# A biased node table made in pieces of 512 nodes at every second pair, read from group 8 on

## The chip, the cores and the metric

The kernel runs on one core of one Trainium2 chip. The metric is device time in microseconds (us); lower is better. The time before the change is 4156.67 us, the median of three runs (4152.97 to 4159.75).

## What is computed

Two graph layers over 6250 nodes of 256 features and 200000 edges, whose destinations are sorted. The change touches the first one:

```python
e = edge_attr @ W_edge + b_edge                 # 200000 x 256
msg = relu(x[src] + e)                          # a gather of node rows
agg = segment_sum(msg, dst, num_segments=6250)
h = relu(((1 + eps) * x + agg) @ W1 + b1) @ W2 + b2   # then batch norm, relu, residual, layer norm
```

The second layer is an attention layer on the result (a gather of rows again, a softmax over each node's edges, a weighted sum). b_edge isn't zero.

## The kernel before

**Tiles, pairs and groups.** The edges are cut into 1563 tiles of 128 edges, one edge on a partition. 14 tiles make a group (112 groups, the last of 9 tiles), and two tiles make a *pair*, seven to a group, 782 in all. The first layer is one loop over the pairs (k from 0), whose order on VectorE (DVE), TensorE (PE), ScalarE (ACT) and SyncE (SP) is the order in which the code is written. GpSimd (POOL) only issues gathers.

**A pair.** `fetch` (L571 on) has POOL issue two indirect DMAs at L576, one for each tile, of 128 rows of 256 floats into a buffer xg; there are 14 such buffers. `features` multiplies the edge attributes by W_edge into PSUM (L586). `sums` adds the gathered rows to it on VectorE (L590) and so releases the xg buffer; `upper` (ScalarE, L595) and `lower` (VectorE, L599) apply the relu and split it into two parts, and `add_up` (TensorE, L609) sums the messages by destination with a one-hot matrix, which `hot` (VectorE, L557) makes for each group. Fetch and features run two pairs ahead of the sum, POOL as far ahead as its buffers and semaphores let it. At each group's end, `flush` runs over the following pairs: totals (L465, L466), and for every two groups the two-layer net and its statistics (L395 to L428).

**The bias.** The bias b_edge can enter in two ways. In groups below GB (XB_FROM = 6) the rows are gathered from the input x, and one more matmul per pair adds the bias (L584, three bf16 rows against a row of ones). In groups from GB on, the rows come from a table xb_tab = x + b_edge in HBM, and that matmul is left out.

**The table.** `first_table` (L515 on) makes it. A step loads 256 nodes from x (L529, SP) into one of three buffers xr, two rows of 1 KB on each partition, 128 nodes apart; then it adds the bias to the piece loaded two steps earlier (L534, VectorE, in place) and writes that piece out (L535, SP). There are 25 pieces (the last has 106 nodes) and 27 steps, one at the end of each pair from k = 4 on.

**What else is in these queues.** SP issues all DMAs that aren't gathers, in the order written, and waits in that order too: every two groups one load of edge attributes ea (L545, 1792 KB), every group a window xw of x (L512, 128 KB), and index loads of 70 KB. There are 13 parts of the indices. `positions` (L137, with the subtraction on VectorE at L131) makes the columns that `hot` needs; its parts 1 to 12 are stepped at every pair from k = 0, two pairs for each part. `order` (loads at L145 and L147, VectorE at L151 to L154) checks the order of the edges; it is stepped at every pair from group GB on. Both take their buffers from the pool ldp, which has two of each kind. `break_columns` (L270) later fills pen_f, a table of 1564 columns.

Of the kernel before, what the change touches and what calls it, by code (L numbers as in the profile page):

```python
# [6 lines left out]
F32 = mybir.dt.float32  # L7
# [4 lines left out]
OP = mybir.AluOpType  # L12
# [6 lines left out]
P = 128  # L19
S = 14  # L20
D = 256
# [8 lines left out]
SLOPE = 0.01  # L30
NEG = -1000.0
BIG = 1e30
XB_FROM = 6
RING = 5
YB = 8
SHORT = 6
# [14 lines left out]
def gnn(ctx, tc, io, N, E):  # L51
    nc = tc.nc
# [4 lines left out]
    GU = NSUB // S  # L57
    GB = min(XB_FROM, G)
    NB = -(-N // P)
# [14 lines left out]
    xb_tab = dram.tile([N, D], F32, name="xb_tab")  # L74
# [14 lines left out]
    be_bc = const.tile([P, D], F32, name="be_bc")  # L89
# [30 lines left out]
    pen_f = const.tile([P, NSUB + 1], F32, name="pen_f")  # L120
    RG = 10
    parts = [(0, 1)] + [(a, min(a + RG, GU)) for a in range(1, GU, RG)]
    parts = [(gs[a], gs[b], first[:, a:b]) for a, b in parts if b <= GU]
# [10 lines left out]
    def positions(r, pool):  # L134
        c0, c1, firsts = parts[r]
        dst_i = pool.tile([P, RG * S], I32, tag="dst_i", name="dst_i")[:, :c1 - c0]
        nc.sync.dma_start(dst_i, io["dst_p"][:, c0:c1])  # L137
        yield
        yield
        minus_first(dloc[:, c0:c1], dst_i, firsts)  # L140
# [40 lines left out]
    def load_rest():  # L181
        if G > 1:
            nc.sync.dma_start(src_sb[:, n0:], io["src_p"][:, n0:])
        nc.scalar.dma_start(w1_sb, io["W1"].rearrange("(k p) f -> p k f", p=P))
        nc.scalar.dma_start(w2_sb, io["W2"].rearrange("(k p) f -> p k f", p=P))
        nc.scalar.dma_start(cols, io["cols"].rearrange("p (a c) -> p a c", c=2))
        nc.scalar.dma_start(ope, io["eps"].partition_broadcast(P))
# [258 lines left out]

    with ExitStack() as st:
        gp = st.enter_context(tc.tile_pool(name="gp", bufs=14))
        ldp = st.enter_context(tc.tile_pool(name="ldp", bufs=2))
        wk = st.enter_context(tc.tile_pool(name="wk", bufs=2))  # L450
        hlp = st.enter_context(tc.tile_pool(name="hlp", bufs=4))
        eap = st.enter_context(tc.tile_pool(name="eap", bufs=2))
# [55 lines left out]
        def window(g):  # L508
            base = nc.values_load(gf_i[:1, g:g + 1], engines=[ET.SP], min_val=0,
                                  max_val=N - 1, skip_runtime_bounds_check_because=IN_RANGE)  # L510
            xw = wk.tile([P, D], F32, tag="xw", name="xw", bufs=3)
            nc.sync.dma_start(xw, io["x"][ds(base, P)])  # L512
            return xw

        def first_table():  # L515

            b_bc = be_bc.unsqueeze(1).to_broadcast([P, 2, D])
            todo = []
            for r0 in range(0, N, 2 * P):
                w = min(2, (N - r0) // P)  # L520
                todo += [(a0, a1, n) for a0, a1, n in
                         ((r0, r0 + w * P, P), (r0 + w * P, min(r0 + 2 * P, N), N % P)) if a1 > a0]
            loaded = []
            for i in range(len(todo) + 2):
                if i < len(todo):
                    a0, a1, n = todo[i]
                    xr = gp.tile([P, 2, D], F32, tag="xr", name="xr", bufs=3)
                    xr = xr[:n, :(a1 - a0) // n]
                    nc.sync.dma_start(xr, io["x"][a0:a1].rearrange("(b p) d -> p b d", p=n))  # L529
                    loaded.append(xr)  # L530
                if i >= 2:
                    a0, a1, n = todo[i - 2]
                    xr = loaded.pop(0)
                    nc.vector.tensor_tensor(xr, xr, b_bc[:n, :(a1 - a0) // n], op=OP.add)  # L534
                    nc.sync.dma_start(xb_tab[a0:a1].rearrange("(b p) d -> p b d", p=n), xr)  # L535
                yield

        def pieces(m):

            t0, t1 = gs[2 * m], gs[min(2 * m + 2, G)]  # L540
            ea_t = eap.tile([P, 2 * SP_], F32, tag="ea", name="ea_t")
            cuts = [0, 2, 8, t1 - t0] if m == 0 else [0, t1 - t0]
            for c0, c1 in zip(cuts, cuts[1:]):
                if c1 > c0:
                    nc.sync.dma_start(ea_t[:, c0 * P:c1 * P], io["eaT"][:, (t0 + c0) * P:(t0 + c1) * P])  # L545
            for t in range(t0, t1):
                EA[t] = ea_t[:, (t - t0) * P:(t - t0 + 1) * P]

        def hot(g):

            n = gs[g + 1] - gs[g]
            OH[g] = ohp.tile([P, S, P], F32R, tag="oh", name="oh")
            h = (n + 1) // 2
            for c0, c1 in ((0, h), (h, n)):
                if c1 > c0:
                    dl = dloc[:, gs[g] + c0:gs[g] + c1]
                    nc.vector.tensor_tensor(OH[g][:, c0:c1], iota_p.unsqueeze(1).to_broadcast([P, c1 - c0, P]),  # L557
                                            dl.unsqueeze(2).to_broadcast([P, c1 - c0, P]), op=OP.is_equal)
                yield
# [52 lines left out]
        K = len(pairs_)  # L612
# [4 lines left out]
        with tc.manual_schedule(engines={ET.DVE, ET.PE, ET.Activation, ET.SP}):  # L617
            def run(gen):
                for _ in gen:
                    pass  # L620

            run(positions(0, ldp))
            pieces(0)
            run(hot(0))
            load_rest()
            XW[0] = window(0)

            side = [positions(r, ldp) for r in range(1, len(parts))]
            rest = [first_table()]
            checks = [order(r, ldp) for r in range(len(parts))]  # L630
            hots, flushes = iter(()), []
            fill = zeros()
            extras = [place_rows(t0, pps, wk) for t0 in range(0, NSUB, P)]
            for f in (0, 1):
                if f < K:
                    fetch(f)
                    features(f)

            def step(queue):
                while queue:  # L640
                    if next(queue[0], True) is None:
                        return True
                    queue.pop(0)
                return False

            for k in range(K + 2):
                g = pairs_[min(k, K - 1)][0]
                if k < K and pairs_[k][1] == 0:
                    hots = hot(g + 1) if g + 1 < G else iter(())
                    if g % 2 == 0 and g + 2 < G:  # L650
                        pieces(g // 2 + 1)
                    if g + 1 < G:
                        XW[g + 1] = window(g + 1)
                    if g == GB - 1:
                        while step(rest):
                            pass
                j = k - firsts_[g] if k < K else 99
                if k + 2 < K:
                    fetch(k + 2)
                    features(k + 2)  # L660
                if k < K:
                    sums(k)
                    upper(k)
                    if 1 <= k:
                        lower(k - 1)
                elif k == K:
                    lower(k - 1)
                if k >= 2:
                    add_up(k - 2)
                    if k - 2 in lasts_:  # L670
                        run(fill)
                        gg = pairs_[k - 2][0]
                        flushes.append(flush(gg, ACC.pop(gg), XW.pop(gg)))
                        if gg > TG and extras:
                            flushes.append(extras.pop(0))
                if k == min(2, K - 1):
                    places_rest()
                if j >= 3:
                    next(hots, None)
                if k < K and pairs_[min(k + 1, K - 1)][0] != g:  # L680
                    run(hots)
                if k < 7:
                    next(fill, None)
                step(flushes)
                if len(flushes) > 1:
                    step(flushes)
                step(side)
                if 4 <= k < K and g < GB:
                    step(rest)
                if g >= GB:  # L690
                    step(checks)
                if k < K and g == TG and pairs_[k][1] == 0:
                    while step(side):
                        pass
                    while step(checks):
                        pass
                    flushes.append(tables(pps, wk))
                    extras = [break_columns(), break_rows(pps, wk)] + extras
            for q in (side, rest, checks, flushes, extras):
                while step(q):  # L700
                    pass
# [678 lines left out]
```

## Time and profile before

| | us |
|---|---|
| median of three runs | 4156.67 (4152.97 to 4159.75) |
| profiled execution, its own time | 4159.51 |
| its span | 4157.7 |
| busy: PE / DVE / ACT / POOL | 2891.7 / 3209.3 / 1029.3 / 3026.7 |
| DMA: read / written | 617.82 MB / 34.99 MB |
| mean granted TensorE clock | 0.824 |

A group line of the profile reads: line, engine, operation, tile written <- tiles read, count | busy us, mean ns of one | idle time of the engine just before them, and what ended it. A line of the timeline has the start, the duration, engine, line, operation, tiles and count, and in brackets the idle time before it with what ended it. A line of the waits has the engine and line that waited, what released it, the total in us, how often, and the longest. A line of the windows has the stretch, then the busy time (and count) of PE, PE's weight loads, DVE, ACT and POOL, the granted clock, the share of the DMA engines that was busy, and GB/s. The suffix q (SPq) marks what an engine's queue issues.

### The profile page before, as it was taken

How to read it: one execution, taken by the hardware profiler on the slowest of the kernel's cores; microseconds unless marked ns; L12 is line 12 of the kernel's file. 1: busy time of each engine (PE TensorE's matmuls, PEld its weight loads, DVE VectorE, ACT ScalarE, POOL GpSimd, SP SyncE). 2: the span in 40 equal slices, each digit the busy share in tenths (PEclk: the TensorE clock that was granted, in tenths of full speed). 3: DMA queues.
4: the chain of work that ended last, by engine and by line, in shares of the span. 5: the costliest groups of instructions: out<-in, count | busy, mean ns of one | idle time of the engine just before them, and what ended most of it. 6: DMA issues, size and time to landing. Idle time of an engine off the chain costs nothing. (4 is left out here: it accounts for less than half of the span.)

```text
span 4157.7 us, 46749 instructions
## 1 busy us (share of the span) xinstructions
PE 2891.7 (70%) x11765; PEld 2091.6 (50%) x11765; DVE 3209.3 (77%) x8203; ACT 1029.3 (25%) x2936; POOL 3026.7 (73%) x3158
## 2 busy tenths in 40 slices
PE   5678777777777777777736666666666666666665
PEld 3466555555566555555524444444444444444443
DVE  5788887777777777777747878787777888777787
ACT  2233333333333333333411111111111111111111
POOL 6577777777777777777457777777777777777773
PEclk8899899999989989999867777777777777777777
DMA  7555555555555555555555555555555555555552
GB/s 248 171 181 183 162 172 168 165 166 166 166 162 165 165 162 162 163 165 164 166 162 142 149 149 150 149 146 145 148 149 149 150 150 145 148 149 148 149 144 69
DMA packets 298114, 656.09 MB, mean 158 GB/s; under 512 B 86923, under 2 KB 170235, under 8 KB 290668
## 3 DMA queue, kind: packets, MB, share of 16 engines
q0 software_dynamic: 150144, 416.54, 36.3%
q1 hardware_dynamic: 146090, 235.43, 16.9%
q8 instruction: 98, 1.61, 0.2%
q14 instruction: 180, 1.47, 0.1%
q10 hardware_dynamic: 1602, 1.04, 0.1%
HBM read 617.82 MB, written 34.99 MB: 157 GB/s over the span
## 5 line engine op out<-in xcount | busy, mean ns | idle before, releaser
L912 POOL DMA_INDIRECT ring<-z_tab,src_sb x1563 | 1509.6, 966 | 495.3 <-issue 300.5
L576 POOL DMA_INDIRECT xg<-xb_tab,src_sb x1479 | 1402.1, 948 | 474.5 <-issue 303.6
L1049 PE MATMUL acc<-y,oh 128*128 128x260 f32 x3126 | 1132.0, 508 | 287.5 <-DVE y L1045 285.6
L586 PE MATMUL pt<-we_sb,ea_t 128*128 128x256 f32 x3126 | 919.4, 420 | 320.9 <-DVE hl L599 315.5
L1049 PEld LDWEIGHTS acc<-y,oh 128*128 128x128 f32 x3126 | 683.6, 242 | 509.4 <-DVE y L1045 387.5
L586 PEld LDWEIGHTS pt<-we_sb,ea_t 128*128 128x128 f32 x3126 | 605.6, 206 | 549.9 <-issue 294.0
L595 ACT ACTIVATE hl<-pt 128x512 fp32r<-128x512 f32 x782 | 467.1, 597 | 1116.7 <-DVE pt L590 1035.0
L590 DVE TENSOR_TENSOR pt<-pt,xg 128x512 f32<-128x512 f32 x782 | 540.6, 691 | 213.1 <-DMA xg<-xb_tab,src_sb 196.8
L609 PE MATMUL acc<-hl,oh 128*128 128x512 f32 x1563 | 690.4, 525 | 3.0 <-ACT hl L595 3.0
L599 DVE SCALAR_TENSOR_TENSOR hl<-pt,hl 128x512 fp32r<-128x512 f32 x782 | 530.8, 679 | 0.5 <-ACT hl L595 0.5
L1045 DVE TENSOR_TENSOR y<-ring,cst 128x520 f32<-128x520 f32 x782 | 520.4, 678 | 2.5 <-PE cst L1017 2.5
L609 PEld LDWEIGHTS acc<-hl,oh 128*128 128x128 f32 x1563 | 322.6, 207 | 55.3 <-ACT hl L595 3.8
L999 PE MATMUL tr<-consts,top 128*4 128x128 f32 x112 | 41.4, 370 | 407.2 <-DVE top L981 407.1
L961 PEld LDWEIGHTS <-ohT 128*128 128x128 bf16 x1563 | 176.8, 116 | 191.0 <-issue 88.6
L1063 ACT COPY ag<-acc 128x260 f32<-128x260 f32 x111 | 41.7, 376 | 868.1 <-DVE acc L1060 868.1
L557 DVE TENSOR_TENSOR oh<-iota_p,dloc 128x896 fp32r<-128x896 f32 x224 | 240.9, 1076 | 0.0
L970 DVE TENSOR_TENSOR oh<-cst,dloc 128x896 f32<-128x896 f32 x224 | 240.5, 1074 | 0.0
L999 PEld LDWEIGHTS tr<-consts,top 128*4 128x4 f32 x112 | 9.2, 82 | 414.8 <-issue 398.5
L989 DVE TENSOR_TENSOR e<-e,ring 128x56 f32<-128x56 f32 x112 | 28.4, 254 | 195.7 <-DMA ring<-z_tab,src_sb 195.0
L961 PE MATMUL pds<-edw,ohT 128*128 128x12 bf16 x1563 | 162.1, 178 | 17.2 <-DMA dlb<-dl_tab 15.2
L422 DVE SCALAR_TENSOR_TENSOR pmk<-p,mk 128x128 f32<-128x128 f32 x224 | 56.3, 289 | 117.9 <-ACT h2T L412 117.9
L395 PE MATMUL p<-hw,w_sb 128*128 128x256 f32 (+1 forms) x456 | 118.5, 384 | 5.2 <-DVE carry L480 4.6
(219 smaller groups left out, 2915.8 us busy)
## 6 DMA issues: line engine op xcount, KB each, us to landing
ea_t<-in_eaT SPq DMA_DIRECT2D x54, 1792.0 KB
dlb<-dl_tab SPq DMA_DIRECT2D x111, 448.0 KB
ring<-z_tab,src_sb POOLq DMA_INDIRECT x1563
xg<-xb_tab,src_sb POOLq DMA_INDIRECT x1479
xw<-in_x SPq DMA_DIRECT2D x112, 128.0 KB
hw<-hT_tab SPq DMA_DIRECT2D x112, 128.0 KB
out<-o SPq DMA_DIRECT2D x110, 128.0 KB
xr<-in_x SPq DMA_DIRECT2D x24, 256.0 KB
```

The lines of the kernel that those rows point to most:

```text
L557: nc.vector.tensor_tensor(OH[g][:, c0:c1], iota_p.unsqueeze(1).to_broadcast([P, c1 - c0, P]), dl.unsqueeze(2).to_broadcast([P, c1 - c0, P] ...
L576: nc.gpsimd.indirect_dma_start(out=XG[k][:, i, :], out_offset=None, in_=io["x"] if g < GB else xb_tab, in_offset=bass.IndirectOffsetOnAxis ...
L586: nc.tensor.matmul(pt[:, i, :], EA.pop(gs[g] + j0 + i), we_sb, start=not g < GB, stop=(not g < GB or i == w - 1))
L590: nc.vector.tensor_add(PT[k][:, :w], PT[k][:, :w], XG.pop(k)[:, :w])
L595: nc.scalar.activation(HL[k][:, :w, 0], PT[k][:, :w], AF.Relu)
L599: nc.vector.scalar_tensor_tensor(HL[k][:, :w, 1], PT.pop(k)[:, :w], 0.0, HL[k][:, :w, 0].bitcast(F32), op0=OP.max, op1=OP.subtract)
L609: nc.tensor.matmul(ACC[g].rearrange("p a d -> p (a d)"), OH[g][:, j0 + i], hl[:, i].rearrange("p a d -> p (a d)"), start=(j0 + i == 0), st ...
L912: nc.gpsimd.indirect_dma_start(out=zg[:, j, :], out_offset=None, in_=z_tab, in_offset=bass.IndirectOffsetOnAxis(ap=src_sb[:, t:t + 1], axi ...
L961: nc.tensor.matmul(pd[:, j].rearrange("p h c -> p (h c)"), ohT[:, j * P:(j + 1) * P], T["edw", g].bitcast(BF16)[:, :3 * H], start=True, st ...
L970: nc.vector.tensor_tensor(T["oh", g][:, c0:c1], iota_p.unsqueeze(1).to_broadcast([P, c1 - c0, P]), dloc[:, gs[g] + c0:gs[g] + c1].unsqueez ...
L1045: nc.vector.tensor_tensor(y[:, :w], T["zg", g][:, j0:j0 + w, :ZW].rearrange("p s (h f) -> p s h f", f=F + 1), by_edge(T["ex", g], g)[:, j0 ...
L1049: nc.tensor.matmul(T["acc", g].rearrange("p h f -> p (h f)"), T["oh", g][:, j0 + i, :], y[:, i].rearrange("p h f -> p (h f)"), start=(j0 + ...
```

## The change

- A piece of the table has 512 nodes (TB = 4), with four neighbouring nodes on a partition, so that a partition's part is one run of 4 KB in x and in the table. There are 12 such pieces and one of 106 nodes, 15 steps.
- A step is made at every second pair, from k = 2 to k = 30.
- Groups 6 and 7 still read x and add the bias on TensorE; the first group that reads the table is 8. The number of gathers from x is 112 instead of 84.
- Two xr buffers of 4 KB on a partition, and the first 1024 columns of pen_f as the third.
- The pool ldp has one buffer of each kind instead of two.
- After the first part, `positions` stands still until the table is done (the second part's load is issued at k = 2 and its subtraction is done after the table); then it goes on at every pair. `order` starts with group 8.

```diff
-XB_FROM = 6
+XB_FROM = 8
+TB = 4
+AHEAD = 2
...
-        ldp = st.enter_context(tc.tile_pool(name="ldp", bufs=2))
+        ldp = st.enter_context(tc.tile_pool(name="ldp", bufs=1))
...
-            b_bc = be_bc.unsqueeze(1).to_broadcast([P, 2, D])
-            todo = []
-            for r0 in range(0, N, 2 * P):
-                w = min(2, (N - r0) // P)
-                todo += [(a0, a1, n) for a0, a1, n in
-                         ((r0, r0 + w * P, P), (r0 + w * P, min(r0 + 2 * P, N), N % P)) if a1 > a0]
+            b_bc = be_bc.unsqueeze(1).to_broadcast([P, TB, D])
+            whole = N // (TB * P) * TB * P
+            todo = [(r0, r0 + TB * P, P, TB) for r0 in range(0, whole, TB * P)]
+            for r0 in range(whole, N, P):
+                todo.append((r0, min(r0 + P, N), min(P, N - r0), 1))
             loaded = []
-            for i in range(len(todo) + 2):
+            for i in range(len(todo) + AHEAD):
                 if i < len(todo):
-                    a0, a1, n = todo[i]
-                    xr = gp.tile([P, 2, D], F32, tag="xr", name="xr", bufs=3)
-                    xr = xr[:n, :(a1 - a0) // n]
-                    nc.sync.dma_start(xr, io["x"][a0:a1].rearrange("(b p) d -> p b d", p=n))
+                    a0, a1, n, b = todo[i]
+                    if i % (AHEAD + 1) == 0 and pen_f.shape[1] >= TB * D:
+                        xr = pen_f[:, :TB * D].rearrange("p (b d) -> p b d", b=TB)
+                    else:
+                        xr = gp.tile([P, TB, D], F32, tag="xr", name="xr", bufs=AHEAD)
+                    xr = xr[:n, :b]
+                    nc.sync.dma_start(xr, io["x"][a0:a1].rearrange("(p b) d -> p b d", p=n))
                     loaded.append(xr)
-                if i >= 2:
-                    a0, a1, n = todo[i - 2]
+                if i >= AHEAD:
+                    a0, a1, n, b = todo[i - AHEAD]
                     xr = loaded.pop(0)
-                    nc.vector.tensor_tensor(xr, xr, b_bc[:n, :(a1 - a0) // n], op=OP.add)
-                    nc.sync.dma_start(xb_tab[a0:a1].rearrange("(b p) d -> p b d", p=n), xr)
+                    nc.vector.tensor_tensor(xr, xr, b_bc[:n, :b], op=OP.add)
+                    nc.sync.dma_start(xb_tab[a0:a1].rearrange("(p b) d -> p b d", p=n), xr)
                 yield
...
-                step(side)
-                if 4 <= k < K and g < GB:
+                if len(side) >= len(parts) - 1 or not rest:
+                    step(side)
+                if 2 <= k < K and k % 2 == 0:
                     step(rest)
                 if g >= GB:
                     step(checks)
```

In the changed kernel the lines stand a little lower: the gather is L580, the bias matmul L588, the sum L594, the table's load, add and write L533, L538 and L539, positions L139 and L133, order L147, L149 and L153 to L156.

## The prediction

> **What bounds the kernel now.** I read the page first. Its line 4, the chain that ended last, says nothing here (four pieces, all at the very end), so I went by part 5 and by the waits.
>
> ```profile
> span 4157.7 us, 46749 instructions
> ...
> L912 POOL DMA_INDIRECT ring<-z_tab,src_sb x1563 | 1509.6, 966 | 495.3 <-issue 300.5
> L576 POOL DMA_INDIRECT xg<-xb_tab,src_sb x1479 | 1402.1, 948 | 474.5 <-issue 303.6
> ```
>
> POOL issues one gather per tile of 128 edges in each layer. A gather takes 0.948 us and about 0.30 us lies between two, so one starts every 1.25 us and a pair every 2.506 us. From 151.72 us to the last gather of the first layer (2003) POOL's timeline has no longer hole: (2002.1 - 153.0) / 738 pairs = 2.506. VectorE (77%) and TensorE (70%) follow POOL there, 3 us behind at the end. So what POOL loses before 151.7 moves the end of the first layer one to one, and the second layer (1563 gathers again) starts that much later. The next views are the windows and POOL's timeline.
>
> ```profile
> 100.00:150.00 50.00, 27.86 (x88) 16.72 (x86) 29.98 (x66) 9.52 (x25) 13.26 (x14) 0.78 0.66 196
> ...
> 200.00:250.00 50.00, 35.30 (x132) 25.10 (x133) 45.91 (x119) 16.00 (x41) 37.81 (x41) 0.93 0.62 199
> ```
>
> ```profile
> 85.16 0.94 POOL L576 DMA_INDIRECT xg<-in_x,src_sb  x1 [4.02 <-DVE pt L590]
> ...
> 126.75 0.95 POOL L576 DMA_INDIRECT xg<-in_x,src_sb  x1 [0.30 <-issue]
> 151.72 0.94 POOL L576 DMA_INDIRECT xg<-xb_tab,src_sb  x1 [24.03 <-DVE oh L557]
> ```
>
> The fifth column of the windows is POOL: 14 gathers in one 50 us, 41 in the other. Two kinds of hole make it. From 85 to 126 us, before the first gather of each of 11 pairs, POOL waits for an xg buffer (released by the sum, L590): 22.4 us together, 19.1 over the usual 0.30 each. Then 24.03 us before the first read of xb_tab, 23.7 over the usual: the last write of the table is issued at 146.5 and has to land; "DVE oh" is only what ended nearby. **Lost: 42.8 us**, and that is all that the change can win in the table's neighbourhood.
>
> Why the table is late is on SP:
>
> ```profile
> SPq L529 <- DMA xb_tab<-xr: 65.9, 22, 10.6
> ```
>
> ```profile
> 88.39 0.37 SPq L529 DMA_DIRECT2D xr<-in_x  x1
> 88.86 0.44 SPq L535 DMA_DIRECT2D xb_tab<-xr  x1
> 92.76 0.37 SPq L529 DMA_DIRECT2D xr<-in_x  x1
> 93.22 0.42 SPq L535 DMA_DIRECT2D xb_tab<-xr  x1
> 96.57 0.37 SPq L529 DMA_DIRECT2D xr<-in_x  x1
> ```
>
> With three buffers, the load of a step waits for the write issued just before it. One step is therefore one write's trip, 3.8 us (92.76 to 96.57), for each pair, against POOL's 2.5 us. VectorE does one add per pair in order, so its sums fall back to 3.8 us a pair, its lag uses up the 14 buffers (pair 30: sum at 135.5, gathered at 80.2), and POOL stops.
>
> **The change part by part.**
>
> *Steps at every second pair, 512 nodes each.* 13 steps of load instead of 25, the same bytes; a step now has two pairs, 5.0 us at POOL's pace. How long is it? No row shows a 512-node step. From below it is today's 3.8 us; from above twice that, 7.7. In between: the added 0.52 MB (load and write) move beside the gathers. The windows give 310 GB/s in 70 to 84 us, where a big ea load runs with the DMA engines 91% busy, and the gathers take 0.26 MB per 2.5 us = 105 of it; 0.52 MB at 205 GB/s is 2.6 us. I take **6.4 us**. The first add stays near 38 us (SP is held until 31.3 by an index load in both kernels); its write lands near 42.7, then nine steps to the last load, 57.6 us, and once an ea load in between (today the step at 72.14 lasts to 84.41: 8.5 us extra). The last load is issued at 109 and the sum of pair 30 runs at about 112. The last write, behind another ea load, lands by about 125.
>
> *First read in group 8.* Its first gather is number 112. On continuous gathers from 80.2 us (pair 30) that is 25 pairs later at 2.506, 143 us plus the port term below. The table is there some 20 us earlier: the 24.0 us wait goes. What is late next is the buffers.
>
> *Buffers.* POOL is held when a sum runs more than 14 x 2.506 - 1.25 - 0.96 = 32.9 us after its gather. Pair 30 in the new order: 112 - 84 = 28 (80.2 us plus some 4 of port delays). Pairs 30 to 56 carry the bias matmul; pairs 31 to 45 today (bias up to 41) took 146.3 to 181.9, 2.54 a pair, so 1 us is added. Pairs 56 to 82 carry the order checks; today's (42 to 68) took 175.9 to 246.1, 2.70 a pair, 5 us added. That is 34 at the worst place: about **1 us** over. With the step at 7.7 us the same sum is 39.5 + 6, 12.6 over; at 3.8 the adds on VectorE decide, 30, nothing over.
>
> *Bias matmuls in groups 6 and 7.* 14 more of L584 at 0.385 us with a weight load of 0.09: 6.7 us of PE, which idles (57% busy from 0 to 150 us). The 2.54 a pair above contains them. Nothing on POOL. If that cover is gone, it is at most 6.7 us.
>
> *The adds.* 24 of 0.69 us become 12 of about 1.25 (two 512-wide pieces of 0.60 and the drain); VectorE's total is unchanged. But look at what an add does to POOL:
>
> ```profile
> 54.24 0.69 DVE L534 TENSOR_TENSOR xr<-xr,be_bc 128x512 f32<-128x512 f32 x1 [1.08 <-DMA xr<-in_x]
> 54.68 1.06 POOL L576 DMA_INDIRECT xg<-in_x,src_sb  x1 [0.31 <-issue]
> ...
> 59.60 0.69 DVE L534 TENSOR_TENSOR xr<-xr,be_bc 128x512 f32<-128x512 f32 x1 [3.21 <-issue]
> 59.81 1.30 POOL L576 DMA_INDIRECT xg<-in_x,src_sb  x1 [0.30 <-issue]
> ```
>
> A gather that starts while an add runs is longer: 0.36 us with 0.48 us of the add left, 0.12 with 0.25 left (54.68, and again at 40.77). So the delay is what is left, less 0.13. Gathers start every 1.25 us, so an add of 1.25 us catches one each time, with 0 to 1.12 us to pay, on average 1.12 x 1.12 / 2 / 1.25 = 0.5: 12 x 0.5 = **6.0 us** on POOL. Between 0 (the starts miss) and 12 x 1.12 = 13.4. Today it paid only 0.6 in the ten adds that met a running POOL. The Trainium skill, SBUF — State Buffer, section Who interferes with whom, has the rule behind this row: a VectorE instruction with two SBUF inputs (as xr and be_bc) contends with a GpSimd instruction that reads SBUF, and the one that comes second is blocked until the first ends. The trace agrees but for the 0.13; by the rule alone the term would be 7.5 and the sum 1.5 us higher.
>
> *Index loads with one buffer, moved behind the table.* Ten of the twelve later loads of positions now stand at pairs 32 to 54 instead of beside the table, and they and the 13 order loads wait for VectorE's read of the load before (L131, L151). VectorE waits for their landing in turn; behind them stand the sums. From one read to the next there are two pairs, 5 us; a trip is the 3.4 us of the table's write or less (70 KB against 256). No stall. It is up to 11.6 us behind an ea load (70.91 to 82.49 us, DVE L131 waiting 9.14 of it). Part 2 needs columns of group 11 at pair 70, and they are there by pair 34. pen_f as third buffer and 4 KB runs cost nothing else: pen_f is first written after group 23 begins, long after the table has landed.
>
> **Sum**, against the profiled execution's own 4159.5 us (span 4157.7 and 1.8 around it): 4159.5 - 42.8 + 6.0 + 1.0 = 4123.7. The profiled one is 2.8 above the median of the runs (4156.67), so by the median it is 4120.9. I forecast 4122, 0.8% below.
>
> **Rivals.**
>
> *The buffers take over* (0.2). The step lasts 7.7 us or more, as twice the bytes would at today's speed; then 12.6 us come back as waits of POOL for L590 between pairs 32 and 82: 4123.7 + 11.6 = 4135. For it: DMA at 0.91 where ea and table meet, and 0.77 to 0.79 in the first 100 us. Against: SP's step is mostly one trip's latency, since the DMA share is 0.66 in 100 to 150 us while it runs.
>
> *The table still isn't there at group 8* (0.05): the change does not do what it is built for, though it reads from group 8. Then a shorter wait stands before the first xb_tab gather. The last write lands some 16 us after the last load's issue, so 149 us needs steps of 9 us (42.7 + 9 x 9 + 8.5 + 16); the sum of pair 30 then runs at 135, the lag is 51, and 18 + 6 us go to the buffers: 4123.7 + 23 = 4147 and up.
>
> *Slower* (0.04). The single-buffered index loads expose their trips on VectorE, at 23 places, each price being the trip less 5 us. It decides once the 23 eat the 5 us of room from a lag of 28 to 32.9 and then the 36 us won: 41 / 23 = 1.8 us each, trips of 6.8 us or more. If all lasted the 11.6 us of the worst row: 23 x 6.6 - 41 = 111 us slower, 4270. Against: only a load behind an ea load shows it, and that comes once in 14 pairs.
>
> *Forecast's own case* (0.71): 4112 (no port delay, 2.8 lower by the median) to 4131 (13.4 of it).
>
> **The numbers.** The range is 4111 to 4144; it takes in the buffer case with steps up to 8.5 us and leaves out the two at the far side. A measurement of this kernel tells about 0.2% (8.3 us) from no change: faster by more 0.92 (the first two cases and the near end of the third), within 0.04 (the rest of the third), slower 0.04.
>
> **What would show it.** Right: POOL's timeline runs through from 80 to 200 us with no hole of over 1 us; its first xb_tab gather near 145 to 151 us shows 0.30 before it; some gathers of 1.3 to 2.1 us stand where an L538 add runs; the second layer's gathers keep 966 ns. Wrong: waits "DVE pt" of several us before gathers at pairs 32 to 82 (buffers), a wait at the first xb_tab gather (table late), VectorE idle before L133 or L153 for DMA (index loads), or SP steps of over 7 us.

## The result and the profile after

The changed kernel takes 4121.73 us, the median of four runs (4119.19 to 4126.10), against 4156.22 for the kernel before (four runs): a ratio of 0.9916, with a 95% interval from 0.9904 to 0.9929. Run again on another chip, its ratio was 0.9930 (0.9916 to 0.9944). The profiled execution took 4121.86 us with a span of 4120.1; the forecast by that scale was 4123.7, on record 4122.

The page first: the two lines of the gathers.

```profile
span 4120.1 us, 46704 instructions
...
L917 POOL DMA_INDIRECT ring<-z_tab,src_sb x1563 | 1509.5, 966 | 495.2 <-issue 304.9
L580 POOL DMA_INDIRECT xg<-xb_tab,src_sb x1451 | 1373.5, 947 | 442.0 <-issue 297.3
```

The second layer is what it was (966 ns). Of the idle time before the first layer's table gathers, 474.5 us became 442.0, though 28 fewer gathers alone make 28 x 0.30 = 8.5 of that; the other 24 are the wait at the switch. The two stretches that stood side by side before are now alike (the fifth number after the comma is POOL, the count behind it its gathers):

```profile
100.00:150.00 50.00, 44.13 (x155) 27.90 (x154) 35.31 (x77) 14.54 (x34) 37.50 (x39) 0.89 0.71 237
200.00:250.00 50.00, 34.48 (x120) 24.17 (x121) 43.59 (x111) 15.57 (x42) 37.87 (x40) 0.84 0.58 173
```

39 gathers in the stretch that had 14. And POOL passes the switch without noticing it:

```profile
150.06 0.95 POOL L580 DMA_INDIRECT xg<-in_x,src_sb  x1 [0.30 <-issue]
151.31 0.95 POOL L580 DMA_INDIRECT xg<-xb_tab,src_sb  x1 [0.30 <-DVE hl L603]
```

On SP, the wait of a load for the write before it is still there, but it is paid 10 times instead of 22, and the step that it makes now serves two pairs:

```profile
SPq L533 <- DMA xb_tab<-xr: 32.2, 6, 8.7
SPq L533 <- DMA xb_tab<-pen_f: 14.2, 4, 5.2
```

```profile
80.16 0.33 SPq L533 DMA_DIRECT2D xr<-in_x  x1
80.54 0.42 SPq L539 DMA_DIRECT2D xb_tab<-pen_f  x1
86.19 0.33 SPq L533 DMA_DIRECT2D pen_f<-in_x  x1
86.61 0.39 SPq L539 DMA_DIRECT2D xb_tab<-xr  x1
```

From 80.16 to 86.19 is a step: 6.0 us, 3.0 a pair, where it was 3.8. What came in exchange is on POOL too:

```profile
59.87 1.22 DVE L538 TENSOR_TENSOR xr<-xr,be_bc 128x1024 f32<-128x1024 f32 x1
59.93 1.97 POOL L580 DMA_INDIRECT xg<-in_x,src_sb  x1 [0.30 <-issue]
```

A gather that starts 0.06 us after an add takes 1.97 us instead of 0.95.

**Where the 37.6 us went**, by the times at which POOL starts its 300th gather (counted from 0, behind all that the change touches): 422.4 us before, 386.8 after, 35.6 won. That is the 42.8 us of holes before, less 7.2 by which ten gathers beside an add are longer, with a few tenths either way (0.6 of the same kind before, two short holes of 0.35). The 300th gather, before and after:

```profile
422.42 0.94 POOL L576 DMA_INDIRECT xg<-xb_tab,src_sb  x1 [0.30 <-DVE pt L590]
386.77 0.94 POOL L580 DMA_INDIRECT xg<-xb_tab,src_sb  x1 [0.30 <-issue]
```

The other 2.0 us come between there and the layer's end, where both kernels only gather: 948 ns a gather against 946. Over all runs here the stretch from gather 300 to 1562 takes 1578.6 to 1582.4 us, in no order with the edits, so this part isn't the change's.

### The profile page after: what moved, and what is told of

It reads as the page before. It is cut to its first block, busy times and chain, and to the rows that moved or that the text cites. A ratio compares the mean times of both kernels' runs of the same rounds, so it can differ in the third digit from the quotient of the medians.

```text
span 4120.1 us, 46704 instructions
## 1 busy us (share of the span) xinstructions
PE 2858.9 (69%) x11779; PEld 2065.1 (50%) x11779; DVE 3205.9 (78%) x8191; ACT 1028.8 (25%) x2936; POOL 3031.0 (74%) x3158
## 5 line engine op out<-in xcount | busy, mean ns | idle before, releaser
L580 POOL DMA_INDIRECT xg<-xb_tab,src_sb x1451 | 1373.5, 947 | 442.0 <-issue 297.3
L1054 PE MATMUL acc<-y,oh 128*128 128x260 f32 x3126 | 1115.9, 502 | 297.4 <-DVE y L1050 294.6
L590 PE MATMUL pt<-we_sb,ea_t 128*128 128x256 f32 x3126 | 905.8, 415 | 325.4 <-DVE hl L603 323.0
L1054 PEld LDWEIGHTS acc<-y,oh 128*128 128x128 f32 x3126 | 674.4, 239 | 517.7 <-DVE y L1050 402.0
L590 PEld LDWEIGHTS pt<-we_sb,ea_t 128*128 128x128 f32 x3126 | 594.2, 203 | 556.5 <-issue 298.8
L594 DVE TENSOR_TENSOR pt<-pt,xg 128x512 f32<-128x512 f32 x782 | 540.9, 692 | 199.0 <-DMA xg<-xb_tab,src_sb 186.3
L613 PE MATMUL acc<-hl,oh 128*128 128x512 f32 x1563 | 678.2, 517 | 3.0 <-ACT hl L599 3.0
L580 POOL DMA_INDIRECT xg<-in_x,src_sb x112 | 113.5, 1014 | 37.0 <-issue 26.5
```

Source lines behind the costliest of these rows:

```text
L580: nc.gpsimd.indirect_dma_start(out=XG[k][:, i, :], out_offset=None, in_=io["x"] if g < GB else xb_tab, in_offset=bass.IndirectOffsetOnAxis ...
L590: nc.tensor.matmul(pt[:, i, :], EA.pop(gs[g] + j0 + i), we_sb, start=not g < GB, stop=(not g < GB or i == w - 1))
L594: nc.vector.tensor_add(PT[k][:, :w], PT[k][:, :w], XG.pop(k)[:, :w])
L613: nc.tensor.matmul(ACC[g].rearrange("p a d -> p (a d)"), OH[g][:, j0 + i], hl[:, i].rearrange("p a d -> p (a d)"), start=(j0 + i == 0), st ...
L1054: nc.tensor.matmul(T["acc", g].rearrange("p h f -> p (h f)"), T["oh", g][:, j0 + i, :], y[:, i].rearrange("p h f -> p (h f)"), start=(j0 + ...
```

## The experiments

For each run the table gives three sums that I added up from POOL's timeline: what gathers beyond 35 us are longer than 0.948 us (those over 1.0 us only); the holes before gathers beyond the usual 0.30 us, at the switch to the table and elsewhere; and the start of gather 300 and of the sum of pair 30. *Held* means: POOL waits for the sum 14 pairs back, which frees its xg buffer; a gather held in this way starts 0.96 us after that sum does. Each run has one profile, so differences of 2 to 3 us between rows can be chance: changed, e2, e10 and e13 run the same code up to pair 40 and have the sum of pair 30 at 106.0 to 108.6 us; e1, e8 and e11 also share theirs and have it at 108.0 to 111.1. Runs of one block shared their runs of the kernel before (4160.5, 4159.4 and 4154.1 us).

| run | median us | ratio (95%) | longer | at the switch | held | gather 300 | sum of pair 30 |
|---|---|---|---|---|---|---|---|
| before | 4156.22 | 1 | 0.9 | 23.7 | 19.1 | 422.4 | 135.5 |
| changed | 4121.73 | 0.9916 (0.9904 to 0.9929) | 7.7 | 0 | 0 | 386.8 | 106.6 |
| e1_bias_psum | 4130.43 | 0.9930 (0.9917 to 0.9943) | 0.3 | 0 | 9.2 | 388.8 | 108.0 |
| e2_from6 | 4141.69 | 0.9962 (0.9949 to 0.9975) | 5.8 | 9.1 | 12.9 | 406.8 | 106.0 |
| e3_old_from8 | 4153.77 | 0.9984 (0.9975 to 0.9993) | 1.5 | 0 | 33.9 | 413.7 | 132.9 |
| e4_old_4buf | 4138.07 | 0.9947 (0.9934 to 0.9960) | 2.6 | 18.5 | 0.6 | 400.8 | 114.7 |
| e5_small_each | 4156.57 | 0.9993 (0.9984 to 1.0002) | 1.9 | 0 | 37.3 | 418.0 | 140.4 |
| e6_1kb_runs | 4129.13 | 0.9929 (0.9915 to 0.9943) | 7.2 | 0 | 1.4 | 387.8 | 107.5 |
| e7_side_on | 4129.43 | 0.9926 (0.9912 to 0.9940) | 5.9 | 0 | 5.6 | 390.2 | 115.5 |
| e8_psum_spread | 4123.20 | 0.9916 (0.9902 to 0.9930) | 0.1 | 0 | 7.0 | 386.1 | 110.2 |
| e10_from6_checks8 | 4131.08 | 0.9943 (0.9929 to 0.9957) | 7.9 | 8.6 | 0 | 394.8 | 106.6 |
| e11_psum_from7 | 4119.62 | 0.9912 (0.9898 to 0.9925) | 0.4 | 2.8 | 5.7 | 388.4 | 111.1 |
| e12_small_4buf | 4126.56 | 0.9931 (0.9917 to 0.9944) | 3.0 | 0 | 8.3 | 389.5 | 114.0 |
| e13_changed | 4125.59 | 0.9930 (0.9916 to 0.9944) | 6.2 | 0 | 3.9 | 389.1 | 108.6 |

My theory: a table step costs the trip of one write, because its load waits for the write issued just before it; carrying two pairs' worth per step brings the table's pace to 3.0 us a pair, and then neither the buffers nor the switch hold POOL. (The trip does depend on what it carries: a step of 256 nodes takes 3.8 us and one of 512 takes 6.0, which is less than twice as much.) The rivals: the later switch does it; the 4 KB runs do it; moving the index loads away does it.

### The later switch alone

```diff
# the kernel before
-XB_FROM = 6
+XB_FROM = 8
```

> The kernel before, but the table is read from group 8 on (nothing else changed). Theory: the 24 us wait for the table turns into waits for xg buffers, because the sums still run at 3.8 us a pair: the gather of pair k can't start before the sum of pair k-14, which puts the first gather of pair 56 at about 180 us instead of 187: 7 us won, 4149. Rival (the wait at the switch was a loss of its own): 24 us won, 4132.

4153.77 us, 0.9984: about 7 us won, as the theory has it. The 24 us wait is gone, and the waits for buffers grow from 19.1 to 33.9 us:

```profile
143.45 0.94 POOL L576 DMA_INDIRECT xg<-in_x,src_sb  x1 [7.37 <-DVE pt L590]
146.34 0.95 POOL L576 DMA_INDIRECT xg<-in_x,src_sb  x1 [0.70 <-DVE pt L590]
162.06 0.94 POOL L576 DMA_INDIRECT xg<-in_x,src_sb  x1 [3.52 <-DVE pt L590]
```

So the longest wait of the profile before was mostly a cover over the next one.

### The larger step: halved, with a fourth buffer, with short runs

```diff
# e5: the changed kernel
-TB = 4
+TB = 2
...
-                if 2 <= k < K and k % 2 == 0:
+                if 2 <= k < K:
```

> The changed kernel with pieces of 256 nodes (two rows, 2 KB, on a partition) at every pair; three buffers, index loads held back and the read from group 8 as in the changed kernel. Theory (a step is one write's trip, whatever it carries): the step is 3.4 to 3.9 us for each pair, the sums fall behind at that pace and POOL is held by buffers for 18 to 28 us between pairs 30 and 90, though the table is there in time: 4138 to 4147. Rival (the longer runs and the index loads out of the way are what counts, not how much a step carries): 4120 to 4126.

4156.57 us, 0.9993: the whole gain is gone, and the time is 10 us above the range that I expected (37.3 us held, not 18 to 28). With the late switch, the 2 KB runs and the index loads out of the way, a step still takes one write's trip, now for one pair:

```profile
93.20 0.33 SPq L533 DMA_DIRECT2D xr<-in_x  x1
93.58 0.43 SPq L539 DMA_DIRECT2D xb_tab<-pen_f  x1
97.41 0.33 SPq L533 DMA_DIRECT2D pen_f<-in_x  x1
97.85 0.37 SPq L539 DMA_DIRECT2D xb_tab<-xr  x1
100.96 0.33 SPq L533 DMA_DIRECT2D xr<-in_x  x1
```

4.2 and 3.6 us. As long as a load waits for the write just before it, nothing is won without the larger step. Is it the size, or the wait? Two runs keep the small pieces and take the wait off by a fourth buffer: a load then waits for the write of the step before last.

```diff
# e4: the kernel before
-                    xr = gp.tile([P, 2, D], F32, tag="xr", name="xr", bufs=3)
+                    if i % 4 == 0:
+                        xr = pen_f[:, :2 * D].rearrange("p (b d) -> p b d", b=2)
+                    else:
+                        xr = gp.tile([P, 2, D], F32, tag="xr", name="xr", bufs=3)
...
# e12: as e5, and
-                    if i % (AHEAD + 1) == 0 and pen_f.shape[1] >= TB * D:
+                    if i % (AHEAD + 2) == 0 and pen_f.shape[1] >= TB * D:
...
-                        xr = gp.tile([P, TB, D], F32, tag="xr", name="xr", bufs=AHEAD)
+                        xr = gp.tile([P, TB, D], F32, tag="xr", name="xr", bufs=AHEAD + 1)
```

> The kernel before with a fourth table buffer (the first 512 columns of pen_f, every fourth piece), so that a load waits for the write of the step before last; pieces of 256 nodes in 1 KB runs at every pair, read from group 6. Theory (a step was one write's trip): steps fall from 3.8 us to 3.1 or less, the pace of VectorE with its add; the sum of pair 30 comes near 110 to 120 instead of 135.5, the first xb_tab gather near 120 to 130 instead of 151.7: 4125 to 4138. Rival (the bytes and the short runs set the step): steps of 3.5 us or more, 4148 or above.

> The run with pieces of 256 nodes at every pair, with a fourth buffer, so that a load waits for the write of the step before last. Theory (not the size of a step but the wait for its own write was the matter): steps of 3.1 us or less, set by VectorE; the sum of pair 30 at 106 to 116 instead of 140.4; 3 to 10 us of buffer waits: 4122 to 4130. Rival (a step has to carry more to pay): steps of 3.5 us or more, 4148 or above.

Both came out by the theory: 4138.07 (22 us won by one buffer: 18.5 where POOL had been held, 19.1 to 0.6, and 5.2 at the switch, less 1.7 of longer gathers) and 4126.56 (ratio 0.9931), against 4156.57 (0.9993) for the same kernel with three. Beside the changed kernel in the same block, e13 with 4125.59, e12 can't be told from it. Five rows of e12:

```profile
81.55 0.33 SPq L533 DMA_DIRECT2D xr<-in_x  x1
81.92 0.44 SPq L539 DMA_DIRECT2D xb_tab<-xr  x1
83.64 0.33 SPq L533 DMA_DIRECT2D xr<-in_x  x1
84.01 0.44 SPq L539 DMA_DIRECT2D xb_tab<-pen_f  x1
...
86.39 0.33 SPq L533 DMA_DIRECT2D xr<-in_x  x1
```

2.1 and 2.8 us. Not all are so short: from the third load on, without the one step in which an ea load stands, the mean step is 2.9 us in e12 (1.7 to 5.8) and 3.0 in e4, against 4.0 in e5 and 4.2 in the kernel before. So pieces of 512 nodes are one way to have a write's trip once for two pairs; another is not to wait for it. Size as such isn't needed.

```diff
# e6: the changed kernel, runs of 1 KB
-                    nc.sync.dma_start(xr, io["x"][a0:a1].rearrange("(p b) d -> p b d", p=n))
+                    nc.sync.dma_start(xr, io["x"][a0:a1].rearrange("(b p) d -> p b d", p=n))
...
-                    nc.sync.dma_start(xb_tab[a0:a1].rearrange("(p b) d -> p b d", p=n), xr)
+                    nc.sync.dma_start(xb_tab[a0:a1].rearrange("(b p) d -> p b d", p=n), xr)
```

> The changed kernel with the four rows of a partition 128 nodes apart, as the kernel before laid them (runs of 1 KB instead of 4 KB). Theory: steps of 6.0 to 6.6 us instead of 6.1; pair 30's sum within 5 us of 106.6; POOL held by 0 to 3 us: 4121 to 4126. Rival (short runs make the transfers slow): steps of 7.5 us or more, pair 30 at 118 or later, 4130 to 4138.

The sum of pair 30 comes 0.9 us later. The median of 4129.13 lies above the expected range, but its ratio of 0.9929 is that of the changed kernel's second set, e13 (0.9930). The steps without an ea load have a mean of 6.4 us, between the 6.2 and 6.7 of the two profiles of the changed kernel. So no gain from the longer runs can be seen.

### The port, and what lies under it

```diff
# e1: the changed kernel; the add's second input in PSUM
-        iota_p = pi.tile([P, P], F32, name="iota_p")
+        psc = pi.tile([P, P + D], F32, name="psc")
+        iota_p, be_p = psc[:, :P], psc[:, P:]
         nc.vector.tensor_copy(iota_p, iota_r)
+        nc.vector.tensor_copy(be_p, be_bc)
...
-            b_bc = be_bc.unsqueeze(1).to_broadcast([P, TB, D])
+            b_bc = be_p.unsqueeze(1).to_broadcast([P, TB, D])
```

> The changed kernel with the bias row that the table's add reads copied once into PSUM, beside iota_p, so that the add has one SBUF input. Theory (port, but covered): the ten gathers of 1.0 to 2.0 us become 0.95 us (7.2 us less on POOL by pair 42), but POOL then meets the buffers, since the changed kernel had only 1.0 us of room at pairs 95 to 97; about 6 us come back as waits for the sum (L594) between pairs 80 and 100, and the time is 4120 to 4122. Rival 1 (the delays simply add up): 4114.5, with no waits for buffers. Rival 2 (the long gathers have another cause than the add's second SBUF input): they stay, 4121.7.

The add takes as long as before (1.21 us), and none of the twelve gathers that start inside an add is longer (0.94 or 0.95 us). One of them:

```profile
56.09 1.21 DVE L540 TENSOR_TENSOR pen_f<-pen_f,psc 128x1024 f32<-128x1024 f32 x1
56.93 0.94 POOL L582 DMA_INDIRECT xg<-in_x,src_sb  x1 [0.30 <-issue]
```

From 35 to 120 us the mean gather is 946 ns in place of 1062. So the cause is the second input from SBUF, as the Trainium skill has it (SBUF — State Buffer, Who interferes with whom). But nothing was won: the median is 4130.43 (4120.93 to 4134.01; 4160.5 before on that chip), 8 us above the expected range and by ratio the changed kernel's. POOL, rid of 7 us of delay, was held 11 times, 9.2 us together, 5.6 of it at pairs 87 to 96. (One more hole, 1.0 us before the first gather of pair 46, is no wait for a buffer: the sum that freed it had started 3.7 us before. What ended it stays open.)

```profile
247.49 0.94 POOL L582 DMA_INDIRECT xg<-xb_tab,src_sb  x1 [1.92 <-DVE pt L596]
248.74 0.94 POOL L582 DMA_INDIRECT xg<-xb_tab,src_sb  x1 [0.30 <-issue]
250.94 0.94 POOL L582 DMA_INDIRECT xg<-xb_tab,src_sb  x1 [1.26 <-DVE pt L596]
```

In the changed kernel the buffer for pair 96 came free 0.04 us before POOL could have used it first (its gather starts 1.00 us after that sum, and 0.96 is the least). In its second profile (e13), where the lengthened gathers took 6.2 us, POOL was held for 3.9 us, all of it at pairs 89 to 96. The port's delay and the wait for buffers are two covers over one limit, the pace of the sums: the sum of pair 82, which frees the buffer for pair 96, starts at 250.6 and 253.0 us in the two profiles of the changed kernel and at 252.7 in e1, port or no port.

```diff
# e8: e1, and
-                if g >= GB:
+                if g >= GB and k % 3 == 0:
                     step(checks)
```

> The run with the bias row in PSUM, and in addition the order checks stepped at every third pair instead of every pair from group 8. Theory (the buffers' room and the port hide each other): without the checks' load on VectorE the waits at pairs 65 to 96 (6.6 of the 10.2 us of that run) go, those at pairs 46 to 52 (2.8) stay; POOL is 4 to 7 us earlier at pair 150 than in the changed kernel, 4115 to 4119. Rival (the buffers hold POOL whatever the checks do): 4121 to 4123.

4123.20 us, above the expected range, and by ratio not to be told from e1 or the changed kernel. Where the edit acts, the theory held: the waits at pairs 87 to 96 (5.6 us in e1) are gone, the sum of pair 82 starts at 244.9 instead of 252.7, and gather 300 comes 2.7 us earlier than in e1, 0.7 ahead of the changed kernel. But the waits at pairs 45 to 66 are 7.0 us instead of 3.6. The edit can't have done that: the first order check stands behind the sum of pair 56, and these waits are for the sums of pairs 31 to 52. For the same reason the expectation was wrong to count on losing the waits at pairs 65 and 66. Up to there e1 and e8 run the same code, with the sum of pair 30 at 108.0 in one and 110.2 in the other, so this is scatter between two profiles, and what the checks cost POOL in the end can't be read from one profile each.

```diff
# e11: e1, and
-XB_FROM = 8
+XB_FROM = 7
...
-                if g >= GB:
+                if g >= 8 and k % 3 == 0:
                     step(checks)
```

> Bias row in PSUM, table read from group 7 on, order checks at every third pair from group 8. Theory (what holds POOL without port delays is the pace of the sums up to pair 66, in which the bias matmul has a part): no wait at the switch (due near 126, table there near 123), 7 bias matmuls fewer, buffer waits 2 to 5 us instead of 6.9: POOL at the 300th gather near 384 to 385 (386.8 in the changed kernel): 4117 to 4121. Rival (the sums' pace is set elsewhere): 4121 to 4124.

The median (4119.62, from 4114.69 to 4128.92) is in the expected range, but not by the expected mechanism: gather 300 starts at 388.4, not 384, the table came 2.8 us late, and 5.7 us were lost to buffers. (The profile is that of the slowest of its five runs, 4128.92.) It has the lowest median of all; its interval (0.9898 to 0.9925) and that of the changed kernel beside it, e13 (0.9916 to 0.9944), overlap. What paces the sums between pairs 10 and 66 stays open.

### The switch at group 6, and the index loads

```diff
# e2: the changed kernel
-XB_FROM = 8
+XB_FROM = 6
```

> The changed kernel, but the table is read from group 6 on. Theory: the table's last write lands near 122 to 124 us and the first read is due at 116, so the first xb_tab gather waits 6 to 9 us; the order checks start 14 pairs earlier. 4126 to 4130. Rival 1 (the later switch is what won the time): a wait of 20 us or more, 4140. Rival 2 (the faster table alone does it, and the 14 bias matmuls cost): no wait, 4117 to 4121.

The wait was as expected, the time was not: 4141.69.

```profile
123.09 0.94 POOL L580 DMA_INDIRECT xg<-xb_tab,src_sb  x1 [9.43 <-issue]
```

12.9 us more were lost between pairs 66 and 82, held for sums. VectorE's waits from 120 to 240 us name it:

```profile
DVE lf L153 <- DMA dnx_i<-in_dnx_p: 17.4, 7, 3.0
...
DVE dloc L133 <- DMA dst_i<-in_dst_p: 5.0, 1, 5.0
```

With the table read from group 6, the order checks start at pair 42, while positions run until 54; both load into the one dst_i buffer, so each load waits for VectorE's read of the other's, and VectorE for each load. This is the mechanism that the prediction had as its case for a slower kernel, at work on a dozen pairs. One more run keeps them apart:

```diff
# e10: e2, and
-                if g >= GB:
+                if g >= 8:
                     step(checks)
```

> The changed kernel with the table read from group 6 on, but the order checks still begin at group 8 (in the earlier run from group 6 they began there too and shared their one index buffer with positions). Theory (two causes in that run: 9 us of wait for the table and 13 us of buffers from index loads that trip over each other): the wait of 8 to 9 us before the first xb_tab gather stays, the buffer waits at pairs 65 to 82 fall under 3 us: 4127 to 4133. Rival (the early switch alone costs it all): 4138 to 4144.

4131.08, by the theory: the wait at the switch stays (8.6 us), nothing else is lost, and the room at pair 96 grows from 0.04 to 9.4 us. By the start of gather 300, the move of the switch to group 8 is worth 6 to 8 us for the table (394.8 against 389.1 and 386.8), and 12 for keeping the two streams of index loads apart (406.8 against 394.8). In time each of the two stands only as a difference of medians, with intervals that overlap.

```diff
# e7: the changed kernel
-                if len(side) >= len(parts) - 1 or not rest:
-                    step(side)
+                step(side)
```

> The changed kernel with positions stepped at every pair from the start, beside the table, as before. Theory: with one buffer for the indices each of these loads makes SP wait for VectorE's subtraction before, and the table's loads stand behind it in SP's order; steps become 1 to 2 us longer, pair 30's sum comes at 112 to 122, POOL is held by 3 to 10 us: 4122 to 4132. Rival (holding them back does nothing): 4119 to 4123.

Positions beside the table put the sum of pair 30 at 115.5, 7 to 9 us later than in the two profiles of the changed kernel, and VectorE waits 11.9 us for index loads up to 150 us. The time (4129.43, 0.9926) can't be told from the changed kernel's, since most of those 9 us are room that is not used: held 5.6 us, against 0 and 3.9. Inconclusive in time. The other parts of the change that move index loads or the table's start, the one buffer in ldp and the first step at k = 2, were not tested alone.

### The changed kernel again

> The changed kernel once more, unchanged, on the chip of these runs, so that the others can be set beside it. All theories: 4117 to 4126; POOL's 300th gather within 1 us of 386.8, some 7 us of lengthened gathers, no hole of over 1 us after pair 2.

4125.59 us. The expectation for the holes failed: held 3.9 us, with up to 1.6 at once, where the first profile had none, and 0.8 us more in one hole at pair 44 whose buffer had long been free. With 0.04 us of room the same kernel lies on either side of the limit from run to run.

## Why the prediction was right

- **42.8 us lost before 151.7 us, all of it to be had.** Right: at gather 300 the changed kernel is 35.6 us ahead (33.3 in its second profile), and the rest is accounted for by the terms below.
- **A step of 6.4 us.** 5.6 to 7.1 us without an ea load, 6.2 on the mean (6.7 in the second profile); the range of 3.8 to 7.7 held it. The step with an ea load in it was over-sized: 9.6 us (64.34 to 73.96), 3.5 extra and not 8.5. The start was 3 us late instead (SP held until 34.6 us, not 31.3). So the sum of pair 30 came at 106.6 and not at 112.
- **The table in time for group 8.** Right, with the room forecast: with the read due at 114 to 116 (e2, e10) it was waited for until 123 to 124, and the read of group 8 came at 151.
- **Buffers, 1 us.** 0 and 3.9 in two profiles. The place was right (the worst lag, 32.9 us at pair 82, just where the checks end; 36.7 in the second profile). That 32.9 is so near to the forecast's 34 is in part luck, since two of its terms were off and cancelled: the lag at pair 30 was 21.5 us (24.3) and not 28, and from there to pair 82 it grew by 11.4 us (12.4) and not by 6. The sums took 2.74 us a pair from 30 to 56 and 2.80 from 56 to 82, where the forecast had 2.54 and 2.70.
- **Port, 6.0 us.** 7.2, at ten of twelve adds. The mechanism was right (e1).
- **6.0 + 1.0 as a sum.** This is the weak step, although the total fitted: the two terms don't add, they replace each other. Without the port (e1) the buffers took 9.2 us. The forecast put the port's delay into the lag, but did not see that the sums' pace sets when the buffers come free either way. In the first profile 7.2 and 0 stood for 6.0 and 1.0, so the sum of the two fitted within 0.2 us by luck. The low end of the forecast's own case, 4112, doesn't follow from its terms either: 4123.7 - 6.0 - 1.0 - 2.8 is 4113.9.
- **Bias matmuls and index loads at nothing.** On POOL's end, yes, in the first profile. On the sums, no: from pair 30 to 56 VectorE runs 11 subtractions of positions (3.1 us) and waits 2.7 us for their loads, and from 56 to 82 it waits 2.7 us for those of order. Together that is 8.5 us, more than the 5.4 us by which the lag grew beyond the forecast; how much of it reached the sums isn't shown. For the bias no run changed only that; e11, with half of the 14 matmuls fewer, shows no gain from it.
- **Rivals.** Buffers: they hold POOL once anything else gives way (e1, e8, e13), but for 4 to 9 us and not by slow steps. The table late: only with the switch at group 6. Slower: the mechanism exists (e2), and the change avoids it by running positions and checks one after the other.

## What to carry to other kernels

A load that reuses the buffer of the write issued just before it turns a pipeline into one trip per step; look at what a load waits for, then give it one more buffer or put more into each step. The longest wait in a profile may lie over a second one, so before removing it ask when the engine could have gone on otherwise. And once several small delays cover the same limit, taking one away shows up in the profile and not in the time.

## What the runs showed of the hardware

A VectorE add with both inputs in SBUF lengthens an indirect DMA that POOL starts while the add runs: 1.22 us of add gave gathers of up to 1.99 us. The gather pays what is left of the add less 0.12 to 0.14 us, in all 19 cases of the changed kernel's two profiles in which 0.18 us or more was left. One exception stands in the kernel before: the gather at 71.43 us, 0.02 us behind the start of an add, took 0.95. One that has already started is not touched: the add at 72.21 us in the changed kernel begins 0.2 us after a gather's start, and that gather took 947 ns. With one input in PSUM the effect is gone, and the add is as long as before. Behind the table the gathers took 946 to 949 ns on the mean from one profile to another, which over a layer makes up to 4 us.
